# Moving z's projections, its SiLU and five products between slots of a selective scan, and fetching raw conv weights a piece earlier

## The chip, the cores and the metric

The kernel runs on one core of one Trainium2 chip. The core has five engines that work side by side, each through its own list of instructions in order: TensorE (PE, matrix products), VectorE (DVE), ScalarE (ACT, activation functions), GpSimd (POOL) and SyncE (SP, which here only issues transfers). They wait for each other through semaphores. The metric is the device time of one launch in microseconds (us), as the median of several runs; less is better.

## What is computed

The input is an image of 64 x 64 positions with 256 channels, in fp32. Cut to what matters here, the reference is:

```
x = x + conv_attention(group_norm(x))     # 1x1, 3x3, 5x5 convs give q, k, v; then a depthwise 3x3, attention, 1x1
t = tokens(x)                             # 4096 x 256
t = t + mamba_both_ways(layer_norm(t))
t = t + experts(layer_norm(t))

def mamba(x):                             # once forwards, once on the reversed tokens
    xc, z = split(x @ in_proj.T)          # 512 channels each
    xc = silu(causal_conv4(xc) + b)
    dt, B, C = split(xc @ x_proj.T)       # 16 columns each
    dt = softplus(dt @ dt_proj.T + db)
    h[t] = exp(dt[t] * A) * h[t-1] + dt[t] * xc[t] * B[t]     # 512 channels x 16 states
    y = (h * C).sum(states) + xc * D
    return (y * silu(z)) @ out_proj.T
```

## The kernel before

Four stages follow each other: the convolutions (`conv_phase`), attention, the two mamba directions (`mamba_phase`) and the experts. In each the order of instructions is written out by hand, engine by engine (`tc.manual_schedule`): what the program emits first, an engine does first. The change touches the first and the third stage.

**Convolutions.** The 3x3 (k) and 5x5 (v) kernels are done by a Winograd-like transform along one axis. A raw weight piece is one row dy of one kernel for one half co of the output channels: three pieces for each half of k, five for each half of v. `load_raw` issues a transfer of a piece into the tile `wr` from GpSimd's queue; `weights` turns it on VectorE into transformed taps, which GpSimd's queue stores to HBM (`uk`, `uv`), from where they come back as `u` for TensorE. The pool `rp` holds one buffer of `wr`. `all_weights` loads a piece, works through it in two or three steps, and then loads the next. It is one of several generators ("fills") whose steps are handed out between the steps of the convolution itself.

**Mamba.** Sixteen passes i: eight chunks of 512 tokens, each in both directions (even i forwards, odd i on reversed tokens). A pass works through 32 slots, numbered `at` = 0 to 31. A slot is two channel groups (j) of one of four tiles e and one of four state quarters k, as one tile of 128 x 1024. For slot n:

- `inflow(n)`, GpSimd (L1671): `dbx` = dt times xc, times B. Three buffers; it is emitted in slot n-2.
- `decay(n)`, ACT (L1661): `da` = exp(dt times A), two instructions into one of two PSUM buffers; emitted in slot n-1.
- `bring(n)`, ACT (L1702): adds a carried state to one column of `dbx`; emitted after `decay(n)`, and in slot 8 also for slot 10.
- `recur(n)`, VectorE: the scan (L1682) and the product `h` = scan times C (L1687). In slots of the set `POOLED` the scan writes `h`, and GpSimd does the product (`pooled`, L1692), emitted one slot later.
- `keep(n)`, ACT (L1710): stores the last column of the scan as state; emitted in slot n+1.
- `sum_states`, TensorE (L1719): sums h over the states into y.
- `close(i, e)`, VectorE (L1727): y times SiLU(z), for a finished tile e; at slots 8, 16, 24 and, for the last tile, slot 0 of the next pass.

Beside this, one step of `prepare(i + 1)` is emitted in each slot (it starts three slots before pass i): the x half of the in-projection (L1249, evacuated by L1276 and L1280) in its first steps, the causal conv, SiLU of xc (L1297) in slot 8, x_proj, softplus in parts, and in slots 24 to 29 the pieces (`dt_piece`, L1364 and L1375 on GpSimd, stores L1379 from SP) that put dt and dt times xc of the next pass into HBM; `load_dt` brings them back as `dtr` and `dtxr`, spread over the partitions. In slots 24 and 26 the z half of the in-projection is emitted, evacuated on ACT in slots 25 and 27 (L1354). The input tile `u` of `prepare` has a single buffer; `load_u` (L1258) brings the next pass's u and is emitted in slot 27, behind that slot's stores in SP's queue. SiLU of z (L1795) stands in slot 0. On even passes from the second on, a tail (layer norm, MLP, second layer norm of a finished chunk) starts in slot 3 and is worked off one step per slot; the table `FULL` lists the slots in which a step for a given engine is held back.

ACT has to load a table when it goes from Exp to SiLU or to Ln and back.

Of the kernel before, what the change touches and what calls it, by code (L numbers as in the profile page):

```python
# [69 lines left out]
def drain(gen):  # L70
    while step(gen):
        pass
# [101 lines left out]
def conv_phase(cx, xT, w1, w3, w5, temp, qd, kd, vd, uk, uv):  # L174
# [17 lines left out]
    with ExitStack() as ctx:  # L192
# [85 lines left out]

        def load_raw(kind, co, dy, pool=rp, tag="wr"):
            n = KS[kind]  # L280
            r = pool.tile([P, 5, C], FP, name="wr", tag=tag)
            nc.gpsimd.dma_start(out=r[:, 0:n, :], in_=RAW[kind][co, :, :, dy, :].rearrange("x p c -> p x c"))
            return r

# [319 lines left out]

        with tc.manual_schedule(engines=ORDERED):
            raw = [load_raw("k", 0, dy, accp, "acc") for dy in range(2)] + [load_raw("k", 0, 2)]
            mv = one.tile([P, CT, 2], FP, name="mv")
            stats = one.tile([P, CT, NCH, 6], FP, name="stats")
            for t in range(CT):
# [39 lines left out]
            for b in range(3):  # L649
                normalise(b)  # L650
            drain(weights("k", 0, 2, raw[2]))
            ready.add(("k", 0))
            first = inputs("k", 0)
            for _ in range(2):
                step(first)
            normalise(3)

            def all_weights(pieces):
                r = load_raw(*pieces[0])
                for n, p in enumerate(pieces):  # L660
                    yield from (True for _ in weights(*p, r))
                    if n + 1 < len(pieces):
                        r = load_raw(*pieces[n + 1])
                    if p[2] == KS[p[0]] - 1:
                        ready.add(p[0:2])

            fills = [
                first, all_weights([("k", 1, dy) for dy in range(3)]), inputs("k", 1),
                all_weights([("v", 0, dy) for dy in range(5)]), inputs("v", 0),
                all_weights([("v", 1, dy) for dy in range(5)]), inputs("v", 1),  # L670
            ]

            pure = fills[1::2]
# [492 lines left out]
def mamba_phase(cx, early, w_in, w_x, w_out, w1, w2, x1d, ud, bcd, dtd, x2d, u2d, usum):  # L1166
# [12 lines left out]
    with ExitStack() as ctx:  # L1179
# [81 lines left out]
        def in_pair(q, e):  # L1261
            return [in_proj(q % 2, gots[q]["u"], e), in_proj(q % 2, gots[q]["u"], e + 1)]
# [4 lines left out]
        def prepare(q):  # L1267

            d, got = q % 2, gots[q]

            ps = in_pair(q, 0)
            yield
            xp = early.wide("xp")
            nc.scalar.copy(xp[:, :, 0:3], halo[d])
            for v in range(2):
                nc.scalar.copy(xp[:, v, 3:], ps[v])  # L1276
            ps = in_pair(q, 2)
            yield
            for v in range(2):
                nc.scalar.copy(xp[:, 2 + v, 3:], ps[v])  # L1280
            nc.scalar.copy(halo[d], xp[:, :, N : N + 3])
            for _ in range(4):
                yield

            xc = None
            for e in range(ET + 1):
                if e > 0:
                    xc = got["xc"] = xc or pr.tile([P, ET, N], FP, name="xc", tag="xc")
                    nc.scalar.activation(xc[:, e - 1, :], ps, AF.Identity, bias=cx.col(f"convb{d}", e - 1))
                if e < ET:  # L1290
                    ps = mm_psum()
                    for k in range(4):
                        nc.tensor.matmul(  # L1293
                            ps, taps[d][:, 4 * e + k, :], xp[:, e, k : k + N], start=k == 0, stop=k == 3
                        )
                yield
            nc.scalar.activation(xc, xc, AF.Silu)  # L1297
            yield
            ps = mm_psum()
            nx = DR + 2 * DS  # L1300
            for e in range(ET):
                nc.tensor.matmul(ps[0:nx, :], wx[d][:, e, :], xc[:, e, :], start=e == 0, stop=e == ET - 1)
            yield
            xd = few()[0:nx, :]
            nc.scalar.copy(xd, ps[0:nx, :])

            at = 0 if d else DR
            nc.sync.dma_start(out=bcd[q], in_=xd[at : at + 2 * DS, :])
            yield


            r = slice(32 * d, 32 * d + DR)
            ex = dt = None
            for e in range(ET + 1):
                if e > 0:
                    ex = early.wide("ex")[:, :, 0:N] if e == 1 else ex
                    dt = dt or sp.tile([P, ET, N], FP, name="dt", tag="dt")
                    nc.scalar.activation(ex[:, e - 1, :], ps, AF.Abs, bias=cx.col(f"dtb{d}", e - 1))
                    nc.scalar.activation(dt[:, e - 1, :], ps, AF.Relu, bias=cx.col(f"dtb{d}", e - 1))
                if e < ET:  # L1320
                    ps = mm_psum()
                    nc.tensor.matmul(ps, wdt[r, P * e : P * e + P], xd[r, :], start=True, stop=True)
                yield

            nc.scalar.activation(ex, ex, AF.Exp, scale=-1.0)
            yield
            rds, sums = {}, {}
            for e in range(ET + 2):
                if e < ET:
                    rd = rds[e] = few()  # L1330
                    nc.scalar.activation(rd, ex[:, e, :], AF.Identity, scale=-1.0, bias=-1.0)
                    nc.scalar.add(rd, rd, 1.0)
                if e > 1:
                    nc.scalar.copy(dt[:, e - 2, :], sums.pop(e - 2))
                if 0 < e <= ET:
                    ps = sums[e - 1] = mm_psum()
                    for v, x in enumerate((rds.pop(e - 1), ex[:, e - 1, :], dt[:, e - 1, :])):
                        nc.tensor.matmul(ps, cx.ident, x, start=v == 0, stop=v == 2)
                yield

            nc.scalar.activation(ex, ex, AF.Ln, bias=1.0)
            yield
            got["dt"] = dt
            for at, (v, e) in enumerate(((0, 0), (1, 0), (0, 1), (1, 1), (0, 2), (0, 3))):
                dt_piece(q, v, e, ex)
                if at == 4 and q > 1:
                    load_first(q, 0)
                if at in (0, 2):
                    zs = in_pair(q, ET + at)
                if at in (1, 3):  # L1350
                    z = sp.tile([P, 2, N], FP, name="z", tag="z", bufs=3)
                    got.setdefault("z", []).append(z)
                    for f in range(2):
                        nc.scalar.copy(z[:, f, :], zs[f])  # L1354
                if at == 3 and q + 1 < 2 * NCH:
                    load_u(q + 1)
                yield
# [66 lines left out]
        def output(i):  # L1424

            c, d = divmod(i, 2)
            g = gots[i]["xc"]
            if d == 0:
                m_of[c] = tl.tile([P, CT, N], FP, name="m", tag="m", bufs=2)
            for co in range(CT):  # L1430
                ps = mm_psum()
                for f in range(ET):
                    nc.tensor.matmul(
                        ps, wout[d][:, f, P * co : P * co + P], g[:, f, :], start=f == 0, stop=f == ET - 1
                    )
                yield
                if d == 0:
                    nc.scalar.copy(m_of[c][:, co, :], ps)
                else:
                    nc.vector.tensor_tensor(m_of[c][:, co, :], m_of[c][:, co, :], ps, ALU.add)  # L1440
            yield
# [283 lines left out]
        def close(i, e):  # L1725
            g, z = gots[i]["xc"], gots[i]["z"]
            nc.vector.tensor_tensor(g[:, e, :], ys.pop((i, e)), z[e // 2][:, e % 2, :], ALU.mult)  # L1727
# [2 lines left out]
        CARRY = {30: (0, 0), 31: (0, 2), 9: (1, 0), 11: (1, 2)}  # L1730


        POOLED = {4, 10, 12, 18, 20, 28}

        AHEAD = 3

        LATE = {0: 0, 1: 0, 2: 0, 3: 0, 4: 0, 7: 5, 13: 2, 14: 2, 15: 2, 16: 2}

        FULL = {
            "PE": {0, 1, 2, 3, 4, 5, 6, 7, 9, 18, 19, 20, 21, 24, 26, 29, 30},  # L1740
            "ACT": {0, 6, 7, 8, 16, 17, 18, 19, 20, 21, 22, 23, 30, 31},
            "POOL": {0, 1, 2, 4, 24, 25, 26, 27, 28, 29, 30, 31},
            "DVE": {8, 16},
# [3 lines left out]
        with tc.manual_schedule(engines=ORDERED):  # L1747
# [5 lines left out]
            for n, (i, e, k, j) in enumerate(slots):  # L1753
# [26 lines left out]
                if j == 0 and n > 0:  # L1780
                    if (n - 2) % SPS not in POOLED:
                        sum_states(n - 2)
                    if k == 0:
                        close(*slots[n - 2][:2])
                        if e == 0:
                            out = output(i - 1)
                if 1 <= at <= 3 and out is not None:
                    step(out)
                    if at == 3:
                        out = None  # L1790
                        if (i - 1) % 2:
                            tails.append(tail((i - 1) // 2))
                if at == 0 and i > 0:
                    for z in gots[i]["z"]:
                        nc.scalar.activation(z, z, AF.Silu)  # L1795
                if i == 0:
# [349 lines left out]
```

## Time and profile before

| | |
|---|---|
| median of 3 runs | 4312.76 us (4305.44 to 4313.22) |
| profiled execution | 4316.87 us |
| its span (first to last instruction) | 4315.0 us |
| convolutions | 0 to about 704 us |
| attention | about 704 to 2040 us |
| mamba | about 2040 to 3993 us (512 scans, from 2044.5 to 3992.6) |
| experts | about 3993 to 4315 us |

| stage | PE busy | DVE busy | ACT busy | POOL busy |
|---|---|---|---|---|
| 0 to 704 | 503.38 | 547.61 | 121.89 | 88.55 |
| 704 to 2040 | 1292.17 | 1091.14 | 1047.11 | 10.50 |
| 2040 to 3993 | 1542.43 | 1776.96 | 1440.47 | 1662.59 |
| 3993 to 4315 | 278.97 | 67.07 | 65.90 | 14.05 |

How to read it: the second table gives the busy microseconds of each engine within a stage. A group line of the profile gives a line of the kernel, the engine, the operation with its tiles, a count, the busy time and mean duration, and after the bar the idle time just before these instructions with what ended it. A timeline row gives start, length, engine, line, operation, and in brackets the idle time before it and its releaser.

### The profile page before, as it was taken

How to read it: one execution, taken by the hardware profiler on the slowest of the kernel's cores; microseconds unless marked ns; L12 is line 12 of the kernel's file. 1: busy time of each engine (PE TensorE's matmuls, PEld its weight loads, DVE VectorE, ACT ScalarE, POOL GpSimd, SP SyncE). 2: the span in 40 equal slices, each digit the busy share in tenths (PEclk: the TensorE clock that was granted, in tenths of full speed). 3: DMA queues.
4: the chain of work that ended last, by engine and by line, in shares of the span. 5: the costliest groups of instructions: out<-in, count | busy, mean ns of one | idle time of the engine just before them, and what ended most of it. 6: DMA issues, size and time to landing. Idle time of an engine off the chain costs nothing. (4 is left out here: it accounts for less than half of the span.)

```text
span 4315.0 us, 43522 instructions
## 1 busy us (share of the span) xinstructions
PE 3617.0 (84%) x15080; PEld 1184.1 (27%) x15080; DVE 3482.8 (81%) x2882; ACT 2675.4 (62%) x4176; POOL 1775.7 (41%) x1148
## 2 busy tenths in 40 slices
PE   4659895999999999998778787878888787876798
PEld 2214341222222222222222222222222222221343
DVE  6887876888888879778899998999999989999211
ACT  1012123888788788776777777777877777774122
POOL 2210000000000000000888888888888889897000
PEclk9879996999999999999888898989899898987799
DMA  4322124000000000002333433433334434432121
GB/s 148 126 81 90 68 91 130 4 20 22 21 26 11 25 22 21 11 18 84 106 114 114 125 121 114 128 114 117 110 106 122 128 114 121 121 110 85 64 64 38
DMA packets 150532, 351.18 MB, mean 81 GB/s; under 512 B 35493, under 2 KB 44453, under 8 KB 150046
## 3 DMA queue, kind: packets, MB, share of 16 engines
q1 hardware_dynamic: 139214, 313.17, 23.6%
q0 software_dynamic: 11088, 35.14, 2.4%
q8 instruction: 120, 1.97, 0.2%
q14 instruction: 110, 0.90, 0.1%
HBM read 268.69 MB, written 79.56 MB: 81 GB/s over the span
## 5 line engine op out<-in xcount | busy, mean ns | idle before, releaser
L1671 POOL TENSOR_TENSOR dbx<-dtxr,b 128x1024 f32<-128x1024 f32 x512 | 1202.1, 2359 | 202.6 <-DVE da L1682 125.4
L959 ACT ACTIVATE e<-sc 128x1024 f32<-128x1024 f32 x1024 | 992.8, 1023 | 205.6 <-PE sc L952 161.4
L1682 DVE TENSOR_TENSOR_SCAN da<-da,state,dbx 128x1024 f32<-128x1024 f32 x416 | 976.7, 2348 | 113.5 <-ACT dbx L1702 66.4
L880 DVE TENSOR_TENSOR s<-s,e 128x1024 f32<-128x1024 f32 x768 | 880.4, 1214 | 43.9 <-ACT e L959 43.3
L1661 ACT ACTIVATE da<-dtr,aneg 128x512 f32<-128x512 f32 x1024 | 708.1, 692 | 59.9 <-DVE h L1682 27.7
L952 PE MATMUL sc<-q,kS 32*128 32x512 f32 x4096 | 653.9, 644 | 21.3 <-DMA kS<-kd 11.5
L132 POOL TENSOR_TENSOR ln_few<-ln_few,minus_half 128x4 f32<-128x4 f32 x29 | 29.4, 1013 | 1415.7 <-DMA ln_few<-ln_row 1415.7
L887 PE MATMUL av<-e,vT 128*32 128x512 f32 x4096 | 549.6, 608 | 3.7 <-ACT o L893 3.7
L1687 DVE TENSOR_TENSOR h<-da,c 128x1024 f32<-128x1024 f32 x416 | 509.4, 1225 | 34.5 <-PE y L1719 4.0
L452 PE MATMUL cv<-v,u 128*128 128x512 f32 x928 | 420.8, 614 | 63.7 <-DVE pad L272 27.2
L1719 PE MATMUL y<-h,sel 128*32 128x512 f32 x2048 | 374.0, 653 | 100.9 <-DVE h L1687 73.5
L1249 PE MATMUL mm<-u,win 128*128 128x512 f32 x496 | 271.8, 704 | 96.3 <-DMA u<-ud 83.9
L952 PEld LDWEIGHTS sc<-q,kS 32*128 32x128 f32 x4096 | 211.3, 184 | 467.7 <-issue 243.4
L452 PEld LDWEIGHTS cv<-v,u 128*128 128x128 f32 x928 | 181.5, 198 | 301.5 <-issue 229.8
L528 DVE SCALAR_TENSOR_TENSOR acc<-pad,wdw_s,acc 128x768 f32<-128x768 f32 (+1 forms) x192 | 244.5, 1279 | 19.4 <-ACT acc L524 13.3
L1682 DVE TENSOR_TENSOR_SCAN h<-da,state,dbx 128x1024 f32<-128x1024 f32 x96 | 224.9, 2343 | 15.5 <-ACT da L1661 6.3
L1692 POOL TENSOR_TENSOR h<-h,c 128x1024 f32<-128x1024 f32 x96 | 226.1, 2355 | 2.1 <-ACT state L1710 2.1
L1293 PE MATMUL mm<-xp,taps 128*128 128x512 f32 x480 | 213.7, 597 | 11.2 <-DVE m L1440 11.2
L1710 ACT COPY state<-da 128x2 f32<-128x2 f32 x415 | 65.3, 157 | 241.4 <-DVE h L1687 240.6
L880 DVE TENSOR_TENSOR s<-e 128x1024 f32<-128x1024 f32 x128 | 150.7, 1217 | 72.1 <-ACT e L959 71.9
L887 PEld LDWEIGHTS av<-e,vT 128*32 128x32 f32 x4096 | 81.3, 108 | 396.8 <-issue 379.2
L1249 PEld LDWEIGHTS mm<-u,win 128*128 128x128 f32 x496 | 108.4, 227 | 267.2 <-issue 147.8
(347 smaller groups left out, 3822.8 us busy)
## 6 DMA issues: line engine op xcount, KB each, us to landing
dtr<-dtd SPq DMA_DIRECT2D x128, 512.0 KB
dtxr<-dtd SPq DMA_DIRECT2D x128, 512.0 KB
b<-bcd SPq DMA_DIRECT2D x64, 256.0 KB
c<-bcd SPq DMA_DIRECT2D x64, 256.0 KB
dtd<-dt SPq DMA_DIRECT2D x64, 256.0 KB
dtd<-few SPq DMA_DIRECT2D x64, 256.0 KB
u<-uv SPq DMA_DIRECT2D x24, 640.0 KB
u<-ud SPq DMA_DIRECT2D x16, 512.0 KB
```

Of the source, the lines that this page charges most:

```text
L452: nc.tensor.matmul(rows4(ps), u[:, dy, P * ci : P * ci + P], v[:, dy : dy + HR, ci, :], start=dy + ci == 0, stop=dy == k - 1 and ci == CT - 1,
L528: nc.vector.scalar_tensor_tensor(o, src, w_ap, o, ALU.mult, ALU.add)
L880: nc.vector.tensor_tensor(z, x, y, ALU.add)
L887: nc.tensor.matmul(g.av[32 * h : 32 * h + 32, :], vT[:, kb, P * t + 32 * h : P * t + 32 * h + 32], es[h // 2][:, h % 2, :], start=kb == 0, ...
L952: nc.tensor.matmul(ps[h // 2][:, h % 2, :], kS[r, t, P * kb : P * kb + P], q_t[r, t, :], start=True, stop=True,)
L959: nc.scalar.activation(e, ps[i], AF.Exp)
L1249: nc.tensor.matmul(ps, win[d][:, t, P * e : P * e + P], u[:, t, ::-1] if d else u[:, t, :], start=t == 0, stop=t == CT - 1,)
L1661: nc.scalar.activation(da[:, v, :], dts[i, e, j][0][:, v, :], AF.Exp, scale=aneg[i % 2][:, a : a + 1])
L1671: nc.gpsimd.tensor_tensor(u, dts[i, e, j][1], bcs[i, k][0][:, None, :].to_broadcast([P, 2, N]), ALU.mult)
L1682: nc.vector.tensor_tensor_scan(das[n].rearrange("p v n -> p (v n)"), da.rearrange("p v n -> p (v n)"), u.rearrange("p v n -> p (v n)"), st ...
L1687: nc.vector.tensor_tensor(h, da, bcs[i, k][1][:, None, :].to_broadcast([P, 2, N]), ALU.mult)
L1719: nc.tensor.matmul(ys[i, e][32 * j : 32 * j + 32, :], cx.sel, hs[n + j // 2][:, j % 2, :], start=False, stop=k == SQ - 1,)
```

## The change

- `wr` gets two buffers in the pool `rp`, and a list `ahead` holds loaded pieces. The first piece of the second half of k is loaded at the very start, the second after the first half's last piece; from then on, when a piece is finished, the piece after the next is loaded.
- The z projections go from slots 24 and 26 to 25 and 27, their evacuation from 25 and 27 to 26 and 28. `FULL["PE"]` holds back tail steps in 25 and 27 where it did in 24 and 26.
- SiLU of z goes from slot 0 to slot 8, where SiLU of xc stands.
- `close(i, 0)` goes from slot 8 to slot 9.
- `POOLED` becomes {0, 4, 12, 18, 28}: slot 0 comes in, slots 10 and 20 go out.

```diff
-            r = pool.tile([P, 5, C], FP, name="wr", tag=tag)
+            r = pool.tile([P, 5, C], FP, name="wr", tag=tag, bufs=2 if pool is rp else None)
...
             raw = [load_raw("k", 0, dy, accp, "acc") for dy in range(2)] + [load_raw("k", 0, 2)]
+            pieces = [("k", 1, dy) for dy in range(3)] + [("v", co, dy) for co in range(CT) for dy in range(5)]
+            ahead = [load_raw(*pieces.pop(0))]
...
             drain(weights("k", 0, 2, raw[2]))
+            ahead.append(load_raw(*pieces.pop(0)))
...
-            def all_weights(pieces):
-                r = load_raw(*pieces[0])
-                for n, p in enumerate(pieces):
-                    yield from (True for _ in weights(*p, r))
-                    if n + 1 < len(pieces):
-                        r = load_raw(*pieces[n + 1])
-                    if p[2] == KS[p[0]] - 1:
-                        ready.add(p[0:2])
+            def all_weights(kind, co):
+
+                for dy in range(KS[kind]):
+                    yield from (True for _ in weights(kind, co, dy, ahead.pop(0)))
+                    if pieces:
+                        ahead.append(load_raw(*pieces.pop(0)))
+                ready.add((kind, co))
...
-                if at in (0, 2):
-                    zs = in_pair(q, ET + at)
                 if at in (1, 3):
+                    zs = in_pair(q, ET + at - 1)
+                if at in (2, 4):
                     z = sp.tile([P, 2, N], FP, name="z", tag="z", bufs=3)
...
-        POOLED = {4, 10, 12, 18, 20, 28}
+        POOLED = {0, 4, 12, 18, 28}
...
-            "PE": {0, 1, 2, 3, 4, 5, 6, 7, 9, 18, 19, 20, 21, 24, 26, 29, 30},
+            "PE": {0, 1, 2, 3, 4, 5, 6, 7, 9, 18, 19, 20, 21, 25, 27, 29, 30},
...
-                    if k == 0:
+                    if k == 0 and at != 8:
                         close(*slots[n - 2][:2])
...
+                if at == 9:
+                    close(i, 0)
...
-                if at == 0 and i > 0:
+                if at == 8 and i > 0:
                     for z in gots[i]["z"]:
                         nc.scalar.activation(z, z, AF.Silu)
```

In this part of `prepare` the variable `at` counts the pieces 0 to 5, which stand in slots 24 to 29.

More of the change, by code (lines that the diff above doesn't have):

```diff
@@ L656, in conv_phase @@
             normalise(3)
-            def all_weights(pieces):
-                r = load_raw(*pieces[0])
-                for n, p in enumerate(pieces):
-                    yield from (True for _ in weights(*p, r))
-                    if n + 1 < len(pieces):
-                        r = load_raw(*pieces[n + 1])
-                    if p[2] == KS[p[0]] - 1:
-                        ready.add(p[0:2])
+            def all_weights(kind, co):
[4 more added lines that the diff above has]
+                ready.add((kind, co))
             fills = [
-                first, all_weights([("k", 1, dy) for dy in range(3)]), inputs("k", 1),
-                all_weights([("v", 0, dy) for dy in range(5)]), inputs("v", 0),
-                all_weights([("v", 1, dy) for dy in range(5)]), inputs("v", 1),
+                first, all_weights("k", 1), inputs("k", 1),
+                all_weights("v", 0), inputs("v", 0),
+                all_weights("v", 1), inputs("v", 1),
             ]
```

## The prediction

> **What bounds the kernel now.** I read first the busy times by stage, then the groups, then the timelines of VectorE, ScalarE, GpSimd and TensorE around the edited slots of passes 8 and 9, then the wait view of the tile `wr`. By stage, the two that are edited (after the length: busy us and instructions of PE, its weight loads, DVE, ACT and POOL, then TensorE's clock, the DMA share and GB/s):
>
> ```profile
> 0.00:704.00 704.00, 503.38 (x1182) 211.13 (x1182) 547.61 (x668) 121.89 (x178) 88.55 (x173) 0.88 0.28 94
> 2040.00:3993.00 1953.00, 1542.43 (x4334) 502.76 (x4332) 1776.96 (x1075) 1440.47 (x2799) 1662.59 (x947) 0.88 0.38 115
> ```
>
> In mamba VectorE (1776.96 of 1953) sets the pace, and GpSimd (1662.59) is close behind it. In the convolutions VectorE leads too, with 156 us idle.
>
> ```profile
> L1671 POOL TENSOR_TENSOR dbx<-dtxr,b 128x1024 f32<-128x1024 f32 x512 | 1202.1, 2359 | 202.6 <-DVE da L1682 125.4
> L1682 DVE TENSOR_TENSOR_SCAN da<-da,state,dbx 128x1024 f32<-128x1024 f32 x416 | 976.7, 2348 | 113.5 <-ACT dbx L1702 66.4
> L1687 DVE TENSOR_TENSOR h<-da,c 128x1024 f32<-128x1024 f32 x416 | 509.4, 1225 | 34.5 <-PE y L1719 4.0
> L1692 POOL TENSOR_TENSOR h<-h,c 128x1024 f32<-128x1024 f32 x96 | 226.1, 2355 | 2.1 <-ACT state L1710 2.1
> ```
>
> A product costs 1.2 us on VectorE or 2.36 on GpSimd. VectorE's remaining loss is waiting before scans. In pass 8 it stands in slots 2, 10 and 21 (first, second and last row); the third row is slot 11 and the fourth slot 12:
>
> ```profile
> 3032.56 2.36 DVE L1682 TENSOR_TENSOR_SCAN da<-da,state,dbx 128x1024 f32<-128x1024 f32 x1 [2.08 <-ACT state L1710]
> ...
> 3063.59 2.35 DVE L1682 TENSOR_TENSOR_SCAN h<-da,state,dbx 128x1024 f32<-128x1024 f32 x1 [0.91 <-ACT state L1710]
> 3065.86 2.33 DVE L1682 TENSOR_TENSOR_SCAN da<-da,state,dbx 128x1024 f32<-128x1024 f32 x1
> ...
> 3069.36 2.34 DVE L1682 TENSOR_TENSOR_SCAN h<-da,state,dbx 128x1024 f32<-128x1024 f32 x1
> ...
> 3101.30 2.36 DVE L1682 TENSOR_TENSOR_SCAN da<-da,state,dbx 128x1024 f32<-128x1024 f32 x1 [1.70 <-ACT dbx L1702]
> ```
>
> A slot with its product on GpSimd lasts 2.27 us (3063.59 to 3065.86), one without 3.50 (to 3069.36): 1.23 apart. Slot 10's wait comes from ACT's trip to the SiLU table and back:
>
> ```profile
> 3057.20 0.29 ACT L1702 ACTIVATE dbx<-dbx,brought 128x1 f32<-128x1 f32 x1 [1.51 <-POOL dbx L1671]
> 3057.51 1.28 ACT L1297 ACT_TABLE_LOAD   x1
> 3058.80 1.91 ACT L1297 ACTIVATE xc<-xc 128x2048 f32<-128x2048 f32 x1
> ...
> 3060.78 1.28 ACT L1661 ACT_TABLE_LOAD   x1
> ```
>
> The trip begins when GpSimd has delivered slot 10's inflow; scan 10 follows 6.08 later (3057.51 to 3063.59).
>
> **Fetching weights ahead.** VectorE waits nine times for a raw piece:
>
> ```profile
>   DMA wr<-in_w: 33.6, 8
>   issue: 5.9, 1
> ```
>
> Three of the nine in the timeline:
>
> ```profile
> 77.98 0.42 DVE L275 TENSOR_TENSOR wx<-wr 128x256 f32<-128x256 f32 x1 [4.76 <-DMA wr<-in_w]
> ...
> 85.14 0.42 DVE L275 TENSOR_TENSOR wx<-wr 128x256 f32<-128x256 f32 x1 [4.69 <-DMA wr<-in_w]
> ...
> 235.20 0.76 DVE L275 TENSOR_TENSOR wx<-wr 128x256 f32<-128x256 f32 x2 [7.08 <-DMA wr<-in_w]
> ```
>
> The one called issue ends 4.9 us after GpSimd issued the load, so it is such a wait too: 39.5 in all. The v pieces stand 11 to 13 us apart (209.79, 222.31, 235.20) and land 3.7 to 8.3 after issue; one piece ahead covers all of that: 0.52 + 5.99 + 5.90 + 1.49 + 7.08 + 5.96 = 26.9 gone. In k's second half the waits are 4.76 and 4.69; the first goes, of the second some 2.9 stays, since its load is issued only when the first buffer is free (73.2, landing 3.7 after a 0.87 issue) and VectorE is there at 75. That is 6.5. The first v piece's wait (3.09) goes, but VectorE then waits as much longer for TensorE's stretch that began at 91.8, behind these weights. What else comes late next? TensorE waits for VectorE by 8.9, 8.4, 3.7, 18.3 and 10.6 us between 140 and 247, 50 in all, so it has room. The load moved to the start joins eight x transfers, with the DMA engines 1.0 busy at 373 to 406 GB/s: 393 KB, +1.0. Sum: -6.5 - 26.9 + 1.0 = **-32.4**, between -39 (all of it) and -15 (TensorE takes over).
>
> **Mamba, per pass.** Slots 10 and 20 take their products back: 2 x 16 x 1.23 = **+39.4**. Slot 0 gives one away, but scan 1 also needs `bring`, which ends 3.6 us after scan 0 starts (in pass 9 at 3145.64, scan 0 at 3142.10). VectorE would be ready at 2.27 plus a gate of 0.6, so only 0.5 is won: 16 x 0.5 = **-8**.
>
> Slot 2's wait is 2.1 in 14 passes; z's table trip that makes it (two loads of 1.283, two SiLU of 1.05) leaves: **-29.4**. In slot 8 one pair of loads then serves both, but z's SiLU, 2.00 for both halves, goes ahead of xc's, so decay 10 and scan 10 come 2.00 later: **+28.0**. The trip's gain on VectorE is thus nearly handed back. The moved gate costs nothing: z's first half is done 2.3 after the trip's start, when VectorE is still in slot 9, and scan 10 behind it waits longer anyway.
>
> The row prices a load at 1.283 with the next activation 0.02 behind it. The Trainium skill (ScalarE: Activation LUTs, What ACT_TABLE_LOAD costs) adds a drain of 1.38 us to each switch; the trace shows none. By the page the trip that leaves would be worth 2.8 more per pass, and the sum some 39 lower.
>
> Slot 0's product also makes the trip start later. From inflow 1 to inflow 10 GpSimd then has ten inflows and two products at 2.33, two pieces (L1375 with L1377) at 1.49 and a tail step of 2.36: 33.3, and 1.0 more for L132 in even passes. Back to back from 1.5 before scan 0, as now, that ends 31.8 (32.8) after it. VectorE reaches slot 8 at today's 30.0 (31.1) less what slots 0 and 2 give back, 27.6 (28.5). With 0.35 for `bring` the trip starts 4.6 after scan 8, where today it is 2.77 in odd passes and 3.75 in even ones: 1.4 on average, 14 x 1.4 = **+19.6**, between 0 and the whole product, 33.
>
> Slot 21's wait is 1.70 because decay 21 waits for scan 20: that wait stands in the built instructions of 15 passes, and it is gone in the changed ones: 14 x 1.70 = **-23.8**. Instead decay 13 waits for scan 12 in six odd passes; priced by the same row, +1.70 each, **+10.2** (0 at best).
>
> **The end of a pass.** Scan 0 of the next pass hangs on a chain: u lands, TensorE projects x, ACT copies, decay, bring.
>
> ```profile
> 3134.48 8.58 PE L1249 MATMUL mm<-u,win 128*128 128x512 f32 x16 [5.94 <-DMA u<-ud]
> ```
>
> Here the move of z's projections counts: 16 rows of L1249 and four copies per pass. u has one buffer, so `load_u` waits for the second pair, now one slot later; behind it on SP are b and c of that slot, first_r, and dtr and dtxr of slot 29. Today u is issued 3.0 to 5.8 after scan 27 starts, by the stores in front of it where GpSimd is late, by the projection elsewhere. In the built order the second pair still stands between the same y sums; it can start when ACT has copied the first, 2.4 to 3.0 into slot 26, and needs 3.7: done 2.7 to 3.5 after scan 27. That is not later than the stores, and these come up to 1.5 earlier in even passes, GpSimd having lost slot 20's product. I take 1.0 per pass, **-14**, between -25 and +49 (a whole slot). The wait of 1.7 in slot 29 of odd passes goes as well, but scan 0 would wait the more; I count nothing. Pass 15 makes its trip for z alone: **+2**.
>
> Mamba: 39.4 - 8 - 29.4 + 28.0 + 19.6 - 23.8 + 10.2 - 14 + 2 = **+24.0**. With -32.4 the whole is -8.4: 4316.9 becomes 4308.5 in a profiled execution. That execution was 4.1 above the median of the runs, so I forecast 4312.8 - 8.4 = 4304. A difference of 0.2% (8.6 us) is about what can be told from none.
>
> **Rivals.**
>
> - Mamba doesn't lose (0.25). If GpSimd keeps up (0 for 19.6), and slot 13's wait is covered, mamba is -6 and the whole -38: 4275. For it: GpSimd idles 202.6 before inflows. Against: the 1.51 in the row of 3057.20, which says it is late now.
> - The u load is late (0.23). If the second z pair ends after the stores, scan 0 moves one for one. It decides from 4.8 us after scan 27; at 2 us beyond that, the -14 becomes +28, and the whole is +34: 4346; at 1 us, 4332. For it: TensorE waits 5.94 for u already. Against: the stores stand in front of u today.
> - TensorE bounds the convolutions (0.12): -15 for -32.4, whole +9: 4322. Against: its 50 us of waits for VectorE.
>
> **How the numbers follow.** The forecast (0.40) covers 4284 to 4316, lower than its middle, because three of its added costs (28.0, 19.6, 10.2) can only fall where an engine waits today. Of it 0.27 lies under 4304.2, 0.12 within 8.6 of 4312.8, 0.01 above. The first rival adds 0.25 to faster, the second 0.23 to slower, the third 0.08 to same and 0.04 to slower. Faster 0.52, same 0.20, slower 0.28. The range 4268 to 4334 takes in the first rival's price and the second's near end.
>
> **What would show it.** Right: L275's waits for `wr` near 3 us, convolutions ending 32 earlier; 28 fewer table loads; no wait in slots 2 and 21; slot 10's wait near 4 us; slot 13's 1.7 in odd passes. Wrong: scan 0's mean wait above today's 2.5, or a mamba stage shorter than 1948 us between its first and last scan.

## The result, and the profile after

The change made no difference that can be told from none. Its median over 12 runs is 4307.8 us (4303.0 to 4313.2), that of the kernel before, over 12 runs, 4310.2 (4301.1 to 4317.0); the ratio is 0.9995 with a 95% interval of 0.9986 to 1.0003. The forecast, 8.4 us less, is a ratio of 0.9981, just below that interval. The profiled executions, against which the sum was made, differ by 8.1 (4316.87 and 4308.75); that of before lay 6.6 above its median, that of the changed kernel 1.0.

That small number is the sum of two large ones. In the profiles the first scan comes 28.2 us earlier (2044.5 to 2016.3), the stretch from the first scan to the last gets 18.7 longer (1945.7 to 1964.4), and what follows 1.5 longer. The line numbers are 2 or 3 higher now: the scan is L1685, its product L1690, `inflow` L1674, `pooled` L1695, `keep` L1713, `bring` L1705, `close` L1730, the y sum L1722, x's and z's projections L1251.

The mamba stage from its first scan to its last, before and then after (columns as in the prediction):

```profile
2044.50:3992.60 1948.10, 1540.26 (x4328) 502.13 (x4328) 1772.26 (x1070) 1438.51 (x2797) 1659.81 (x946) 0.88 0.38 115
2016.30:3983.10 1966.80, 1540.27 (x4328) 500.87 (x4328) 1790.09 (x1086) 1402.80 (x2765) 1620.89 (x929) 0.86 0.38 114
```

ScalarE and GpSimd have less to do there, 36 and 39 us, and it did not help. The groups of the page:

```profile
L1674 POOL TENSOR_TENSOR dbx<-dtxr,b 128x1024 f32<-128x1024 f32 x512 | 1202.4, 2358 | 217.6 <-DMA dtxr<-dtd 94.1
...
L1685 DVE TENSOR_TENSOR_SCAN da<-da,state,dbx 128x1024 f32<-128x1024 f32 x432 | 1014.3, 2348 | 79.6 <-ACT da L1664 39.6
...
L1685 DVE TENSOR_TENSOR_SCAN h<-da,state,dbx 128x1024 f32<-128x1024 f32 x80 | 187.4, 2343 | 58.4 <-PE y L1722 54.6
```

Durations are the same to within 1 ns. What is new is the last figure: scans that write `h` wait 54.6 us for y sums on TensorE. The largest waits of VectorE in the mamba stage (total, times, longest), first before, then after:

```profile
DVE da L1682 <- ACT dbx L1702: 66.4, 38, 4.5
DVE da L1682 <- ACT state L1710: 30.2, 16, 2.1
```

```profile
DVE h L1685 <- PE y L1722: 54.6, 13, 6.8
DVE da L1685 <- ACT da L1664: 39.6, 12, 4.9
DVE da L1685 <- ACT state L1713: 25.6, 9, 3.8
DVE da L1685 <- ACT dbx L1705: 10.3, 20, 1.1
```

Of the rows after, the first is scan 0, and the second and third are mostly scan 10. In pass 8 the wait of scan 0 looks like this, on VectorE and on TensorE:

```profile
2999.98 2.35 DVE L1685 TENSOR_TENSOR_SCAN h<-da,state,dbx 128x1024 f32<-128x1024 f32 x1 [1.90 <-PE y L1722]
```

```profile
2990.08 8.80 PE L1251 MATMUL mm<-u,win 128*128 128x512 f32 x16 [2.00 <-ACT ln_rstd L125]
2998.81 1.92 PE L1722 MATMUL y<-h,sel 128*32 128x512 f32 x16
```

Both x projections, 16 matmuls, stand ahead of the y sums of the last slots, and scan 0 starts when the first eight of these are done. `h` has four buffers, so slot 0 writes into the one that slot 28 used, and only these sums free it. Slot 8 of the same pass, on ScalarE and then on VectorE (scan 8 starts at 3027.59):

```profile
3031.93 0.29 ACT L1705 ACTIVATE dbx<-dbx,brought 128x1 f32<-128x1 f32 x1 [2.01 <-POOL dbx L1674]
3032.23 1.28 ACT L1800 ACT_TABLE_LOAD   x1
3033.52 2.00 ACT L1800 ACTIVATE z<-z 128x1024 f32<-128x1024 f32 x2
3035.43 1.89 ACT L1299 ACTIVATE xc<-xc 128x2048 f32<-128x2048 f32 x1
...
3037.39 1.28 ACT L1664 ACT_TABLE_LOAD   x1
```

```profile
3040.20 2.36 DVE L1685 TENSOR_TENSOR_SCAN da<-da,state,dbx 128x1024 f32<-128x1024 f32 x1 [3.61 <-ACT state L1713]
```

The trip again starts when GpSimd has delivered inflow 10, now 4.6 after scan 8 in this pass.

The stretch between two scans, taken from their starts in the two traces and summed over the 16 passes, splits mamba's 18.7 by slots:

| where | forecast | measured |
|---|---|---|
| slot 10's product back | +19.7 | +21.5 |
| slot 20's product back, slot 21's wait gone | 19.7 - 23.8 = -4.1 | -4.7 |
| slot 0's product away | -8 | -21.3 |
| slot 2's wait gone | -29.4 | -30.7 |
| slots 8 and 9: z's SiLU (28.0), late trip (19.6) | +47.6 | +41.3 |
| slot 13's wait, odd passes | +10.2 | +5.7 |
| slots 24 to 31, up to scan 0 | -14 + 2 | +6.0 |
| all others | 0 | +0.9 |
| sum | +24.0 | +18.7 |

### The profile page after: what moved, and what is told of

It is laid out like the page before. It is cut to its first block, busy times and chain, and to the rows that moved or that the text cites. A ratio compares the mean times of both kernels' runs of the same rounds, so it can differ in the third digit from the quotient of the medians.

```text
span 4306.9 us, 43517 instructions
## 1 busy us (share of the span) xinstructions
PE 3611.1 (84%) x15080; PEld 1183.7 (27%) x15080; DVE 3502.2 (81%) x2898; ACT 2641.7 (61%) x4148; POOL 1739.1 (40%) x1132
## 5 line engine op out<-in xcount | busy, mean ns | idle before, releaser
L1674 POOL TENSOR_TENSOR dbx<-dtxr,b 128x1024 f32<-128x1024 f32 x512 | 1202.4, 2358 | 217.6 <-DMA dtxr<-dtd 94.1
L1685 DVE TENSOR_TENSOR_SCAN da<-da,state,dbx 128x1024 f32<-128x1024 f32 x432 | 1014.3, 2348 | 79.6 <-ACT da L1664 39.6
L132 POOL TENSOR_TENSOR ln_few<-ln_few,minus_half 128x4 f32<-128x4 f32 x29 | 29.4, 1014 | 1414.2 <-DMA ln_few<-ln_row 1414.2
L1690 DVE TENSOR_TENSOR h<-da,c 128x1024 f32<-128x1024 f32 x432 | 529.1, 1225 | 33.9 <-PE mm L1340 0.5
L452 PE MATMUL cv<-v,u 128*128 128x512 f32 x928 | 420.5, 614 | 58.7 <-DVE pad L272 21.4
L1722 PE MATMUL y<-h,sel 128*32 128x512 f32 x2048 | 369.8, 656 | 91.0 <-DVE h L1690 70.4
L1251 PE MATMUL mm<-u,win 128*128 128x512 f32 x496 | 269.2, 698 | 90.2 <-DMA u<-ud 64.3
L1713 ACT COPY state<-da 128x2 f32<-128x2 f32 x431 | 68.2, 158 | 301.5 <-DVE h L1690 300.7
L1685 DVE TENSOR_TENSOR_SCAN h<-da,state,dbx 128x1024 f32<-128x1024 f32 x80 | 187.4, 2343 | 58.4 <-PE y L1722 54.6
L1695 POOL TENSOR_TENSOR h<-h,c 128x1024 f32<-128x1024 f32 x80 | 188.4, 2355 | 7.0 <-ACT state L1713 7.0
L1304 PE MATMUL mm<-xc,wx 128*48 128x512 f32 x120 | 88.6, 908 | 112.6 <-ACT state L1713 108.2
```

The lines of the kernel that those rows point to most:

```text
L452: nc.tensor.matmul(rows4(ps), u[:, dy, P * ci : P * ci + P], v[:, dy : dy + HR, ci, :], start=dy + ci == 0, stop=dy == k - 1 and ci == CT - 1,
L1251: nc.tensor.matmul(ps, win[d][:, t, P * e : P * e + P], u[:, t, ::-1] if d else u[:, t, :], start=t == 0, stop=t == CT - 1,)
L1674: nc.gpsimd.tensor_tensor(u, dts[i, e, j][1], bcs[i, k][0][:, None, :].to_broadcast([P, 2, N]), ALU.mult)
L1685: nc.vector.tensor_tensor_scan(das[n].rearrange("p v n -> p (v n)"), da.rearrange("p v n -> p (v n)"), u.rearrange("p v n -> p (v n)"), st ...
L1690: nc.vector.tensor_tensor(h, da, bcs[i, k][1][:, None, :].to_broadcast([P, 2, N]), ALU.mult)
L1722: nc.tensor.matmul(ys[i, e][32 * j : 32 * j + 32, :], cx.sel, hs[n + j // 2][:, j % 2, :], start=False, stop=k == SQ - 1,)
```

## The experiments

Each ratio is to the kernel before on the same chip; the kernels ran on several chips. "Scans" is the stretch from the first scan's start to the last one's in one profiled execution (before 1945.7, after 1964.4).

| kernel | ratio, 95% interval | scans, us |
|---|---|---|
| changed | 0.9995 (0.9986 to 1.0003) | 1964.4 |
| fetch-ahead alone | 0.9928 (0.9913 to 0.9943) | 1945.5 |
| slot 0 not pooled | 0.9915 (0.9899 to 0.9930) | 1936.4 |
| y sum of 28 earlier | 0.9973 (0.9962 to 0.9983) | 1949.2 |
| SiLU of z back | 0.9933 (0.9918 to 0.9948) | 1938.2 |
| old set | 0.9933 (0.9919 to 0.9946) | 1935.3 |
| z projections back | 1.0009 (0.9998 to 1.0021) | 1963.2 |
| product 4 moved to 10 | 0.9957 (0.9943 to 0.9971) | 1940.4 |
| {4, 10, 12, 18, 28} | 0.9893 (0.9878 to 0.9908) | 1916.8 |
| the same, SiLU of z back | 0.9874 (0.9859 to 0.9889) | 1908.6 |
| and slot 24 pooled | 0.9974 (0.9965 to 0.9984) | 1943.9 |
| and slot 26 pooled | 0.9922 (0.9909 to 0.9936) | 1932.6 |
| and slot 28 not pooled | 0.9918 (0.9903 to 0.9933) | 1931.9 |

### The two halves

The first edit of the diff alone, on the kernel before.

> The kernel before with the fetch-ahead alone; mamba as before. Theory: the two halves of the change are independent, and the first scan came 28.2 us earlier in the changed kernel (2044.5 to 2016.3), so this one is 28 us shorter than before, about 4282, with the distance from the first to the last scan unchanged at 1946 to 1948. Rival: the time won in the convolutions is partly lost in attention or in mamba whatever mamba looks like (a lower granted clock where the engines rest less): then under 20 us shorter, 4290 or more, with a longer mamba stage although its instructions are those of before.

It is 0.72% faster, 31 us, with the first scan 27.8 earlier and the stretch of scans unchanged. Nothing is given back in attention or mamba, and the granted clock is not lower (0.913 to 0.917, beside 0.909 to 0.914 before). So the mamba half costs 0.9995 / 0.9928, which is 0.67% or 29 us; the profiles have 18.7 and the forecast had 24.0.

### Slot 0 out of the set

```diff
-        POOLED = {0, 4, 12, 18, 28}
+        POOLED = {4, 12, 18, 28}
```

> The changed kernel with slot 0 taken out of POOLED, nothing else. Theory: slot 0's product costs time at two places away from slot 0. A scan that writes h needs its h buffer at its start, and slot 28's h is only released by a state sum that stands on TensorE behind the second x projection of the next pass, so scan 0 starts 2.05 us per pass later than it would (4.50 instead of 2.45 after the start of the second copy into xp); and GpSimd is 1.4 us later at slot 8. Slot 0 itself gets 1.34 longer. Net 2.1 us per pass: 4275 to 4282, the table trip in slot 8 starting 2.8 to 3.8 us after scan 8, scan 0's mean wait under 3. Rival: scan 0 waits because u is late, and GpSimd's lateness at slot 8 has another source: then only slot 0 changes, +21, about 4329.

The ratio is 0.80% below the changed kernel's, and the profile says where: slot 0 gets 21.3 longer, scan 0 comes 28.2 earlier over all passes (slot 31), slots 8 and 9 give 15.3, slots 3 and 7 another 5.8. From the first x projection on TensorE to scan 0 it takes 8.1 us in passes 2 to 14, where the changed kernel takes 10.05 and the kernel before 8.1. The trip starts 3.8 after scan 8 (passes 3 to 14) instead of 5.0. So a product taken from VectorE made the kernel slower at two other places, in front of scan 0 and in slot 9.

### The y sum of slots 28 and 29 ahead of x's second pair

```diff
-                if j == 2 and n > 2 and (n - 3) % SPS in POOLED:
+                if j == 2 and n > 2 and (n - 3) % SPS in POOLED - {28}:
                     sum_states(n - 3)
...
-                    if (n - 2) % SPS not in POOLED:
+                    if (n - 2) % SPS not in POOLED - {28}:
                         sum_states(n - 2)
```

> The changed kernel with the state sum of slots 28 and 29 emitted in slot 30, ahead of the second x projection, where it stood behind it in slot 31. Theory of the h buffer: scan 0 no longer waits for the second x projection and starts 2.45 us after the start of the second copy into xp, 2.05 earlier than now; scan 1 then waits more for its bring, behind the copies of the second pair (slot 0 gets 0.8 longer, toward 3.6). Net 1.2 us per pass, 19 in all: about 4289. Rival, late u: scan 0's releaser becomes the copy of x and its start does not move: 4308.

TensorE's queue and scan 0 in pass 8:

```profile
2984.34 3.67 PE L1251 MATMUL mm<-u,win 128*128 128x512 f32 x8 [0.96 <-DMA u<-ud]
2987.94 1.07 PE L1722 MATMUL y<-h,sel 128*32 128x512 f32 x8
2988.93 3.70 PE L1251 MATMUL mm<-u,win 128*128 128x512 f32 x8
2992.57 1.09 PE L1722 MATMUL y<-h,sel 128*32 128x512 f32 x8
```

```profile
2992.46 2.34 DVE L1685 TENSOR_TENSOR_SCAN h<-da,state,dbx 128x1024 f32<-128x1024 f32 x1
...
2996.50 2.36 DVE L1685 TENSOR_TENSOR_SCAN da<-da,state,dbx 128x1024 f32<-128x1024 f32 x1 [1.12 <-ACT dbx L1705]
```

The eight sums now stand between the two pairs, and scan 0 waits for nothing in this pass. Over passes 1 to 15 its mean wait falls from 3.7 to 1.4, and none of it is for y sums. So it was the `h` buffer, not u. Slot 31 gives 35.4, more than the 31 expected; slot 0 takes 22.1 back, not 12, since scan 1 now waits for its `bring`. The ratio moves by 0.22%, 10 us, half of what was expected: the mechanism is shown, its worth was overrated. (This profile is the fastest of its 12 runs.)

### SiLU of z back in slot 0

```diff
-                if at == 8 and i > 0:
+                if at == 0 and i > 0:
                     for z in gots[i]["z"]:
                         nc.scalar.activation(z, z, AF.Silu)
```

The gate of tile 0, `close(i, 0)`, goes back to slot 8 with it.

> The changed kernel with SiLU of z back in slot 0 and the gate of tile 0 back in slot 8. Theory: the table trip for z costs about as much beside that of x as by itself, since 2.0 us of SiLU stand in slot 8 in front of decay 10: slots 8 and 9 get 2.0 shorter (28 us over 14 passes), and slots 0 and 1 get 1.5 to 2.1 longer (21 to 29 us): 4300 to 4310, no change. Rival: slot 10 waits for GpSimd's late inflow anyway, so the 2.0 there are hidden and the move was worth the whole 29: 4330 or more.

The theory and the rival were both wrong: it is 0.62% faster than the changed kernel, 27 us, and 26.2 in the stretch of scans. Slots 0 to 2 get 26.6 longer, as expected, but slots 8 and 9 get 35.8 shorter, slot 12 gives 8.2 and slot 31 6.8. The expectation priced the 2.0 us of SiLU and left out what the prediction had counted: what VectorE wins in slot 2 it waits for GpSimd in slot 8. With that win gone the trip starts 3.9 after scan 8 and not 5.0.

### The old set, and slot 4's product moved behind the trip

```diff
-        POOLED = {0, 4, 12, 18, 28}
+        POOLED = {4, 10, 12, 18, 20, 28}
```

> The changed kernel with the old POOLED, {4, 10, 12, 18, 20, 28}; everything else changed. Against the profile of the changed kernel: slot 0 +21, scan 0 -28 and slot 9 -15 as without slot 0 in the set; slot 10 -21.5; slots 20 and 21 +5 (a product less, the wait of 1.70 back), slots 12 and 13 -6, the wait of slot 29 in odd passes +11. Together -33: about 4275, a ratio to before of 0.992. So the new set would have cost what the fetch-ahead won. Rival: GpSimd is the bound of the mamba stage as a whole, and seven... six products instead of five make it late further on: 4290 or more.

The ratio is 0.62% below the changed kernel's, and the stretch of scans 29.1 shorter (33 expected). So the new set costs about what the mamba half costs, and the other two moves together change nothing that can be told by the ratios (0.9933 beside 0.9928 for the fetch-ahead alone); the two profiles, from two chips, differ by 10.2 in the scans.

The next one has {0, 10, 12, 18, 28}: each engine has as many products as in the changed kernel.

> The changed kernel with slot 10 in POOLED for slot 4: {0, 10, 12, 18, 28}. Each engine has as many products as in the changed kernel; one has been moved from in front of the inflow that the table trip in slot 8 waits for to behind it. Theory (between inflow 1 and inflow 10 GpSimd sets the pace): slot 4 gets 1.23 longer and slot 10 as much shorter, and of the 3.6 by which GpSimd then stands better against VectorE at slot 8 only the lateness over 3.4 comes back, 5.0 to 3.4: 1.6 per pass over 14 passes, 23 in all: a ratio to before of 0.994, the trip 3.4 to 3.8 after scan 8. Rival: the order of GpSimd's products does not matter, only their number: ratio 0.9995, the trip still 5 after scan 8.

The trip starts 3.8 after scan 8 and not 5.0; the stretch of scans is 24.0 shorter, 10.6 of it in slot 31 and not only in slot 9; the ratio is 0.38% below the changed kernel's, 16 us. It matters in front of which inflow GpSimd has its product.

### z's projections back

> The changed kernel with z's projections back in slots 24 and 26, their evacuation in 25 and 27, and the table of held-back slots with them. Theory: u was issued 4.4 us after scan 27 on average, 4.5 before the change, so the place of the projections is nearly without effect: within 10 us of the changed kernel, 4298 to 4312. Rival: the projection one slot later is what makes scan 0 late (its wait grew from 2.3 to 3.8): 20 to 30 less, 4280.

Within 10 us, as expected: scans 1.2 shorter, the ratio 0.14% higher with overlapping intervals. Scan 0 waits 1.1 less and slot 28 is 12.9 longer, since slot 29's wait in odd passes is back: the same delay, one place earlier.

### A better set

The set {4, 10, 12, 18, 28} in the changed kernel, and the same with SiLU of z in slot 0.

> The changed kernel with POOLED = {4, 10, 12, 18, 28}: as without slot 0, and slot 10's product back on GpSimd, slot 20's not. Theory (GpSimd is late only between inflow 1 and inflow 10, and has room behind it): a further 1.25 to 1.35 per pass, 20 to 22 less than the set {4, 12, 18, 28}: ratio to before 0.986 to 0.988, no wait in slots 13 and 21. Rival: GpSimd is late behind slot 10 as well, and the product of 2.36 comes back as waits for inflows in slots 11 to 13: under 8 less, ratio 0.990 or more.

> The same set {4, 10, 12, 18, 28}, with SiLU of z in slot 0 and the gate of tile 0 in slot 8. With slot 0 in the set, SiLU of z in slot 8 cost 26. Theory: 2.0 in slot 8 against 2.1 in slot 2 is an even exchange, and the 26 came from GpSimd's lateness alone (what VectorE won in slot 2 it waited for in slot 8): without slot 0 in the set the two places of SiLU are within 8 of each other. Rival: the trip in slot 8 is on the path in any case and dearer than the one in slot 0: this kernel is faster by 15 to 26 than the one with SiLU in slot 8.

The first is 19.6 shorter in the scans than {4, 12, 18, 28}, slot 10 alone by 19.2; by the ratios, on two chips, 0.22%. In the scans that is nearly the 20 to 22 that were expected; the ratio of 0.9893 lies between the two ranges. Slot 13's wait of 1.1 stayed in odd passes, against the expectation. The second is 8.2 shorter again: slots 0 to 2 longer by 26.0, slots 8 and 9 shorter by 24.6, slots 12 and 13 by 8.1. With slot 0 unpooled the move of SiLU is the even exchange that was forecast, but for slot 13. This is the best kernel of the study, 1.26% faster than before, and its mamba stage, first scan to last, beside that of the changed kernel (1966.80 us, in the section on the result) shows what it is made of:

```profile
2013.80:3924.80 1911.00, 1534.13 (x4328) 499.37 (x4328) 1790.08 (x1086) 1437.51 (x2793) 1622.42 (x929) 0.88 0.38 117
```

VectorE has the same 1086 instructions and the same 1790.1 us in both, GpSimd the same 929. The 55.8 between them is idle time of VectorE.

### The end of a pass

Three more sets on that kernel: slot 24 added, slot 26 added, slot 28 taken out.

> The set {4, 10, 12, 18, 28} with SiLU of z in slot 0, and slot 24 pooled as well. By the room on VectorE it is worth 1.23 per pass, 20: ratio to before 0.983. Against it: GpSimd has six pieces of 1.3 to 1.5 to do in slots 24 to 29 beside its inflows and runs there back to back; if the pieces, their stores and u, which stands behind them in SP's queue, come up to 2.36 later, scan 0 of the next pass takes back 15 and more of it: 0.987 or above.

> The same with slot 26 pooled instead of 24. Same two theories; closer to the pieces, so a smaller gain than slot 24's if GpSimd is what counts there (ratio 0.988 or above), and the same 0.983 if it is not.

> The set {4, 10, 12, 18} with SiLU of z in slot 0: slot 28's product taken from GpSimd as well, which in slots 24 to 29 also has the six pieces in front of u. Theory: with a product more there (slots 24 and 26 pooled) u was issued 6.5 and 7.6 us after scan 27 instead of 4.6; with one less the stores are earlier, u is issued near 3.5, and scan 0 takes back what slot 28 loses (1.27 per pass, 20): ratio to before 0.985 to 0.988. Rival: u is no longer held by GpSimd's pieces there, but by the second z projection, which stays: u at 4 or later, and the product costs its 20: 0.991 to 0.992.

Adding a product cost 1.0% and 0.5%, on the side of the second theory and by more than it said. u is issued 6.5 and 7.6 us after scan 27 (passes 2 to 14), where it was 4.6, and slot 31 takes 37.9 and 32.7: from scan 27 to scan 0 it is 21.0 and 20.9 instead of 18.4. Slot 24 won only 5.3, because scan 25 then waits 1.7 in even passes. Slot 26 cost less than slot 24, where the reverse was expected: its product won 20.3 in its own slot, and x's projection followed u's issue by 4.9 instead of 6.1. SyncE's queue in pass 7, without slot 24 (scan 27 at 2950.09) and with it (2968.39):

```profile
2953.28 0.43 SPq L1382 DMA_DIRECT2D dtd<-few  x1
2954.68 0.32 SPq L1260 DMA_DIRECT2D u<-ud  x1
```

```profile
2973.09 0.43 SPq L1382 DMA_DIRECT2D dtd<-few  x1
2973.57 0.47 SPq L1260 DMA_DIRECT2D u<-ud  x1
```

With slot 24 pooled the store is issued 4.7 after scan 27 instead of 3.2, and u goes straight behind it; without, u has a gap of 1 in front of it, in which it waits for z's second projection (that ends 0.03 before u is issued), as it does in every other pass. So the last experiment, taking a product out, had little to win: with slot 28's product gone u is issued at 4.3 instead of 4.6, the product costs its 21.4, and the ratio is the rival's 0.992. Slot 31 gives 13.7 of that back, not by an earlier scan 0 (18.7 after scan 27, beside 18.4 with slot 28 pooled) but because VectorE comes to it later and waits less; slots 0 and 1 cost 12.3 more.

## Why the prediction came out as it did

The range held the time and the sum was near the profiles' difference, but through errors that cancelled, which is luck; and "no difference", which had a chance of 0.20, is what the runs show.

- **Convolutions, -32.4, measured -28.2** (first scan), 31 by the ratio. The waits for `wr` fell from 39.5 to 4.2, one of them the 2.60 that was to stay as some 2.9:

```profile
  DMA wr<-in_w: 2.6, 1
  issue: 1.6, 1
```

  The v pieces gave what was forecast; what failed are the terms in front of them, -6.5 + 1.0. By 70.8 VectorE was 2.5 late and not 1.0, 1.4 of it from waits for x at the start and the rest from waits for `c`:

```profile
68.27 1.29 DVE L275 TENSOR_TENSOR out_t<-cv,c 128x512 f32<-128x512 f32 x2 [5.54 <-ACT c L481]
```

```profile
70.79 1.29 DVE L275 TENSOR_TENSOR out_t<-cv,c 128x512 f32<-128x512 f32 x2 [5.92 <-ACT c L481]
```

  And the wait behind the first v piece, which was said to grow by 3.09, grew by 7.3:

```profile
105.17 1.29 DVE L275 TENSOR_TENSOR out_t<-cv,c 128x512 f32<-128x512 f32 x2 [2.48 <-ACT c L481]
```

```profile
104.89 1.29 DVE L275 TENSOR_TENSOR out_t<-cv,c 128x512 f32<-128x512 f32 x2 [9.78 <-ACT c L481]
```

  The first of each two is before, the second after. All that VectorE had won up to there it waited for here, and it is 0.3 ahead; at the last v piece's row (269.83 before, 242.09 after) it is 27.7 ahead. TensorE's stretch, on which this row waits, begins at the same time in both:

```profile
91.80 18.72 PE L452 MATMUL cv<-v,u 128*128 128x512 f32 x38 [13.89 <-DMA u<-uk]
```

```profile
91.74 18.50 PE L452 MATMUL cv<-v,u 128*128 128x512 f32 x38 [11.30 <-DMA u<-uk]
```

  The first of the taps for it was issued 2.5 earlier (88.45 and 85.95). Why they landed no earlier no run shows.
- **Slot 0, -8, and the end of the pass, -14: two wrong steps of opposite sign.** The prediction let scan 0 keep its releaser. A scan that writes `h` needs the buffer at its start, and slot 28's is freed by a y sum behind x's second pair. So the wait in front of scan 1 moved to scan 0: slot 0 got 21.3 shorter instead of 8, and slots 24 to 31 got 6.0 longer instead of 12 shorter. The sign that the prediction set itself, scan 0's wait above 2.5, was there: 3.7 on average over passes 1 to 15, where the trace of before has 2.3.
- **u.** It was said to be issued 1.0 earlier; the mean went from 4.5 to 4.4 after scan 27, so nothing. (With the fetch-ahead alone, where mamba is that of before, it is 5.3, so a difference of 0.7 between two traces says little here.) But x's first projection, which waits for u, starts 10.6 after scan 27, where it was 11.8 before and 12.2 with the fetch-ahead alone. That is about the 1.0 of the forecast by another way, and what made it so no run shows. From there to scan 0 the `h` buffer then cost 1.9. The rival of a late u did not occur, and the slot of z's projections hardly matters. The sets with slots 24 and 26 show that rival's mechanism, set off by GpSimd.
- **GpSimd's lateness, +19.6, right.** The trip starts 5.0 after scan 8, where 4.6 was forecast. (In odd passes 30.0 less 0.5 and 2.1 is 27.4, not 27.6; that makes it 4.7.) The first rival, that GpSimd keeps up, fell. The prediction did not say that by its own -8 and +19.6 slot 0 was a loss already. Measured, its product won 21.3 in slot 0 and cost 15.3 in slots 8 and 9, 5.8 in slots 3 and 7 and 28.2 in front of scan 0.
- **z's trip, -29.4 against +28.0, right as a pair** (slot 2 gave 30.7): without slot 0 in the set the two places are worth the same within 8.2 us. With slot 0 in the set the move alone cost 26.2. The 28 table loads that went (101 to 73 in the trace) bought nothing that shows. A load still takes 1.28 with the next activation 0.01 behind it (3032.23, 3033.52). The drain that the Trainium skill (ScalarE: Activation LUTs, What ACT_TABLE_LOAD costs) adds to a switch shows in no row here.
- **Slot 13's wait** was priced by slot 21's 1.70 and is 1.05 to 1.06 in the six odd passes.

What stays open: the ratios price the mamba half at 29, the profiles at 19. Part of that may be that the profile of before was 6.6 above its median; one execution of each cannot say which slots hold the rest.

## What to carry to other kernels

- An engine that looks busy on average need not be what to relieve: in front of each wait, see which engine comes last there. Moving a product to an engine that is late at the next meeting point, or behind whose late result the buffer hangs, can cost more than the product, as slot 0's did here.
- When the place of a result changes from the second instruction of a step to the first, its buffer is needed earlier; follow that buffer back to what frees it, through the queue of the engine that does so.
- Time that two engines win in front of a common meeting point counts once. Price each edit by the wait that is left at the next such point, not by the one it removes.

## What was not expected of the hardware

Nothing new of an engine's speed: the same instruction took the same time in all kernels (2.35 for a scan, 2.36 for a product on GpSimd). Single profiled executions of one kernel can be far from its median, 4293.5 against 4307.0 for the kernel with the earlier y sum, so a profile's stage sums carry some 10 us of uncertainty here.
